# One more product of the setup by nested Strassen, in a new order, and four sums of W1 moved

## The chip, the cores and the metric

The kernel runs on one core of a Trainium2 chip. The metric is the time of one execution on the device in microseconds (us), the median of a few runs. Engines: TensorE (PE in the profile, its weight loads PEld), VectorE (DVE), ScalarE (ACT), GpSimd (POOL) and SyncE (SP), which issues most of the DMAs. All data are 32-bit floats.

## The reference

Shapes: x is 8 x 1024 x 1024, the context 8 x 64 x 512; D = 1024.

```python
mp = einsum('bme,de->bmd', ctx, W_mem)                 # 8 x 64 x 1024
scores = einsum('bnd,bmd->bnm', x, mp) / sqrt(D)
attn = softmax(scores)
mc = einsum('bnm,bmd->bnd', attn, mp)
gate = sigmoid(concat([x, mc], -1) @ W_gate.T + b_gate)
out = rmsnorm(x + gate * mc, norm_w)
```

With W_gate.T cut into an upper half W1 (for x) and a lower half W2 (for mc), the argument of the sigmoid is x W1 + attn (mp W2) + b. The kernel multiplies mp by W2 once, in the setup, and adds b there.

## The kernel before, in words

**Setup** (the first 79 us of the span). The context and W_mem come in, TensorE multiplies them by Strassen's scheme into mp transposed, kept as four tiles `m11, m12, m21, m22` of 128 x 4 x 256. Then mp W2 is formed by Strassen's scheme in Winograd's form, with seven products, into `c11, c12, c21, c22`, which go to DRAM (`store_mg`). Its left operands are `m11`, `m12`, `m22` and the sums `s1 = m21 + m22`, `s2 = s1 - m11`, `s3 = m11 - m21` and a fourth in s2's place; its right operands are the quarters `b11..b22` of W2 and sums of them: `t1 = b12 - b11`, `t2 = b22 - t1`, `b12` replaced by `b22 - b12`, `b21` replaced by `b21 - t2`. The products are:

1. m11 b11, 2. m12 b21 (the plain one), 3. (m12 - s2) b22, 4. m22 b21 (the replaced one), 5. s1 t1, 6. s2 t2, 7. s3 b12.

A dense product (`mg_product`) is 8 matmuls of 512 columns into two PSUM banks. Product 5 is nested (`second_product`): it is itself done by the same scheme, 7 inner products of two 256-column matmuls, with four sums of left quarters (`second_left`, on VectorE, tile `mg_left`), four sums of right quarters (`second_sum`, on GpSimd, tile `mg_right`), copies between banks on ScalarE and two adds into the banks on VectorE. A function given as `between` is issued ahead of the last inner product. The order before is 1, 5, 2, 6, 7, 4, 3. PSUM bank pairs are `up`, `side` and `both` (in the profile `pm_af`, `pm_ed` and `pm_ctx` in some order, with `mg_u` for the two inner banks). Product 1 is needed in most results: it is copied to `both`, and product 6 is accumulated on it.

In the same stretch VectorE and GpSimd make the weights of the main part: `outer_sum` (a sum of two 128 x 2048 quarters of W1, VectorE) and `inner_sum` (128 x 512, mostly GpSimd), which fill the `t{o}` and `it{o}` tiles; and the first quad of x is transposed on VectorE (`transpose_x`).

**Main part.** x is worked on in 16 quads of 512 rows. For each quad x W1 is formed by seven outer products in the order `ORDER = (1, 6, 7, 5, 4, 2, 3)`, each nested into seven inner products (banks `af`, `ed`, `kB`, `kC`). After the third inner product of outer products 4 and 3 stand the visits, which add attn (mp W2) (`pc`). Other work is laid in by hand: `at(slot, ...)` puts it ahead of the inner product of that number (49 to a quad), `mid((q, o, n), ...)` at places inside an outer product; `mid((0, 4, 0), ...)` comes right after the visits of outer product 4 of the first quad. The left sums of the next outer product (`inner_s`) are made on GpSimd. Each engine takes its instructions strictly in the order in which the program issues them (`keep_in_program_order`), and an instruction that waits holds up all behind it on its engine. All `tensor_tensor` sums carry line 96 and all matmuls line 93 in the profile, since one helper issues them.

Of the kernel before, what the change touches and what calls it, by code (L numbers as in the profile page):

```python
# [8 lines left out]
F32 = mybir.dt.float32  # L9
# [11 lines left out]
def tile_gated_cross_attention_rmsnorm(  # L21
# [73 lines left out]
    def tt(eng, o, a, b, op):  # L95
        pin(eng.tensor_tensor(o, a, b, op))  # L96
# [51 lines left out]
    def load_xq(q):  # L148
        b, n0 = q // QPB, (q % QPB) * QT
        xq[q] = t4k(xqpool, [P, 16, Q4], "xq", f"xq{q}")  # L150
        src = x[b, n0 : n0 + QT, :].rearrange("(s c) (i e) -> i c s e", c=32, i=4)
        for i in range(4):
            load(xq[q][32 * i : 32 * (i + 1), :, :], src[i])
# [58 lines left out]
    def outer_sum(o, a, b, k=slice(0, 4)):  # L212
        tt(nc.vector, outer_b[o][:, k], outer_b[a][:, k], outer_b[b][:, k], ALU.subtract)

    def inner_sum(eng, o, n):
        s, a, b = ((T1, R12, R11), (T2, R22, T1), (R12, R22, R12), (T4, R21, T2))[n]
        tt(eng, w_op(o, s), w_op(o, a), w_op(o, b), ALU.subtract)

    def inner_sums(eng, o):
        w1_place(o)  # L220
        for n in range(4):
            inner_sum(eng, o, n)
# [94 lines left out]
    def w2_sum(eng, o, a, b):  # L317
        for k in range(KH):
            tt(eng, o[k], a[k], b[k], ALU.subtract)

    def second_right(r, tag):

        r11, r21 = (r[:, 2 * k : 2 * k + 2, 0:C] for k in range(2))
        r12, r22 = (r[:, 2 * k : 2 * k + 2, C:H] for k in range(2))
        t = const.tile([P, 3, 2, C], F32, tag=tag, name="mg_right")
        return r11, r21, r12, r22, *(t[:, i, :, :] for i in range(3))

    def second_sum(eng, right, n):
        r11, r21, r12, r22, t4, t1, t2 = right
        o, a, b = ((t1, r12, r11), (t2, r22, t1), (t4, r21, t2), (r12, r22, r12))[n]  # L330
        tt(eng, o, a, b, ALU.subtract)

    right5 = second_right(t_w2[0], "it3")
    for k in range(KH):
        tt(nc.gpsimd if k > 1 else nc.vector, t1[k], b12[k], b11[k], ALU.subtract)
    for n in range(3):
        second_sum(nc.gpsimd, right5, n)
    w2_sum(nc.gpsimd, t2, b22, t1)
    second_sum(nc.gpsimd, right5, 3)
    pm_sum(m22, m22, up)  # L340
    outer_sum(5, 7, 1)
    w2_sum(nc.gpsimd, b12, b22, b12)
    inner_sums(nc.gpsimd, 1)

    pm_product(both, ps4, e22)
    pm_copy(m21, both)
# [190 lines left out]
    def store_mpT(r, h):  # L537
        load(mpd[:, h * KH : (h + 1) * KH, r * HM : (r + 1) * HM], mpT[r][h])
# [4 lines left out]
    def mp_step(eng, tag, pool, a, b, op):  # L543
        t = t4k(pool, [P, KH, HM], tag, f"mp_{tag}")
        tt(eng, t, a, b, op)
        return t
# [14 lines left out]

    def first_rows():

        t = const.tile([P, 2, Q4], F32, tag="it4", name="rows0")
        for h in range(2):
            pin(
                nc.vector.transpose(
                    chunks(t, KD)[:, h * KH : (h + 1) * KH], mpT[0][h][:, :, 0:M]
                )
            )  # L570
        store_rows(0, t)
# [10 lines left out]
    def mg_product(l, r, pgs, start=False):  # L582
        for t in range(2):
            for k in range(KH):
                mm(pgs[t], l[:, k, t * P : (t + 1) * P], r[k], start and k == 0, k == KH - 1)

    def second_left(eng, l, tag):

        l11, l12, l21, l22 = quarters(l)
        t = const.tile([P, 5, 2, P], F32, tag=tag, name="mg_left")  # L590
        s1, s2, s3, s4, zs = (t[:, i, :, :] for i in range(5))
        tt(eng, s1, l21, l22, ALU.add)
        tt(eng, s2, s1, l11, ALU.subtract)
        tt(eng, s3, l11, l21, ALU.subtract)
        tt(eng, s4, l12, s2, ALU.subtract)
        return l11, l12, l22, s1, s2, s3, s4, zs.rearrange("p k c -> p (k c)")

    def second_product(left, right, pgs, between):

        l11, l12, l22, s1, s2, s3, s4, zs = left  # L600
        r11, r21, r12, r22, t4, t1, t2 = right
        top, low = pgs
        u2 = bank("b", [P, C], "mg_u2")
        z = u3 = bank("c", [P, C], "mg_u3")

        def product(o, l, r, start=False):
            for k in range(2):
                mm(o, l[:, k, :], r[:, k, :], start and k == 0, k == 1)

        product(u2, l11, r11, True)  # L610
        pin(nc.scalar.copy(top[:, 0:C], u2))
        product(z, s1, t1, True)
        pin(nc.scalar.copy(zs, z))
        product(u2, s2, t2)
        pin(nc.scalar.copy(u3, u2))
        product(top[:, 0:C], l12, r21)
        tt(nc.vector, top[:, C:H], u2, zs, ALU.add)
        product(u3, s3, r12)
        pin(
            nc.scalar.copy(  # L620
                low.rearrange("p (n c) -> p n c", c=C), u3.unsqueeze(1).to_broadcast([P, 2, C])
            )
        )
        product(top[:, C:H], s4, r22)
        between()
        product(low[:, 0:C], l22, t4)
        tt(nc.vector, low[:, C:H], low[:, C:H], zs, ALU.add)

    def mg_tile(pool, tag, name):
        return t4k(pool, [P, 2, H], tag, name)  # L630

    def mg_copy(o, pgs):
        for t in range(2):
            pin(nc.scalar.copy(o[t] if isinstance(o, list) else o[:, t, :], pgs[t]))
# [5 lines left out]
        )  # L640

    s1 = mp_step(nc.vector, "s1", apool, m21, m22, ALU.add)
    store_mpT(0, 1)
    load_xq(0)
    c11 = mg_tile(rot, "u", "mg_c11")
    c12 = mg_tile(rot, "u", "mg_c12")
    c21 = mg_tile(rot, "l2", "mg_c21")
    c22 = mg_tile(small, "mg", "mg_c22")
    up, side = side, up
    mg_product(m11, b11, up, True)  # L650
    mg_copy(both, up)
    left5 = second_left(nc.vector, s1, "it6")

    def left6():
        nonlocal s2
        s2 = mp_step(nc.vector, "s2", apool, s1, m11, ALU.subtract)

    s2 = None
    second_product(left5, right5, side, left6)
    mg_copy(c22, side)  # L660
    outer_sum(7, 3, 7)
    w1_place(7)
    for n in range(4):
        inner_sum(nc.gpsimd, 7, n)
    mg_product(m12, b21, up)
    mg_copy(c11, up)
    store_mg(c11, 0, 0)
    first_rows()
    load_mp(0)
    s3 = mp_step(nc.vector, "junk", small, m11, m21, ALU.subtract)  # L670
    for t in range(4):
        transpose_x(0, t, 0)
    for part in range(2):
        inner_s(0, 1, part)
    w2_sum(nc.vector, b21, b21, t2)
    mg_product(s2, t2, both)
    mg_copy(c21, both)
    tt(nc.gpsimd, s2, m12, s2, ALU.subtract)
    for t in range(2):
        tt(nc.vector, side[t], c21[:, t, :], side[t], ALU.add)  # L680
# [94 lines left out]
    for n in (2, 3):  # L775
        at(4, inner_sum, nc.gpsimd, 4, n)
    for i, (o, n) in enumerate((o, n) for o in (2, 3) for n in range(4)):
        if i > 5:
            mid((0, 4, 0), inner_sum, nc.vector, o, n)
        else:  # L780
            at((3, 4, 5, 6, 14, 14)[i], inner_sum, nc.vector, o, n)
    slot = 0

    def step():
# [412 lines left out]
```

## Time and profile before

| what | us |
|---|---|
| median of 3 runs (945.33 to 946.3) | 946.27 |
| the profiled execution | 946.12 |
| its span | 943.5 |
| TensorE busy | 932.2 |
| VectorE busy | 803.7 |
| GpSimd busy | 738.1 |
| ScalarE busy | 432.6 |
| first matmul of the main part starts at | 78.88 |

How to read it: the span runs from the first to the last instruction of the profiled execution; its own time holds 2.6 us more around the span. Times in rows are microseconds from the start of the span. Matmuls are pipelined, and each row's duration reaches past the start of the next, so the time of a product is read from start to start.

### The profile page before, as it was taken

What the parts mean: (1) busy time and instruction counts of PE and PEld (TensorE: products, weight loads), DVE (VectorE), ACT (ScalarE), POOL (GpSimd) and SP (SyncE); (2) the same over time, 40 slices, a digit from 0 to 9 for tenths busy, and PEclk for the clock granted to TensorE, in tenths of its full rate; (3) what the DMA queues carried; (4) which work ended last, traced back from release to release, by engine and by line L of the source; (5) the groups of instructions that cost most, each with busy time, mean ns of one, the idle gap of its engine ahead of it and who ended that gap; (6) DMA issues with size and microseconds to landing.
All of it is one profiled execution on the core that took longest, in us unless ns stands there. A gap on an engine that the chain in (4) does not pass through costs nothing.

```text
span 943.5 us, 15920 instructions
## 1 busy us (share of the span) xinstructions
PE 932.2 (99%) x5572; PEld 727.7 (77%) x5572; DVE 803.7 (85%) x1267; ACT 432.6 (46%) x1111; POOL 738.1 (78%) x814
## 2 busy tenths in 40 slices
PE   9999999999999999999999999999999999999995
PEld 8646778787877778787877778687877778787774
DVE  6798988888897888888897888888897889888887
ACT  4212336273644527263644627263543627264556
POOL 4998978689686868778696868778696868878695
PEclk9999999999999999999999999999999999999998
DMA  9927294582919365481919366491918466491632
GB/s 378 310 69 157 47 162 115 125 178 51 206 57 185 103 137 125 118 183 44 214 57 179 90 145 135 101 201 33 221 60 168 101 136 144 93 205 31 137 151 89
DMA packets 71183, 128.43 MB, mean 136 GB/s; under 512 B 12608, under 2 KB 49472, under 8 KB 70848
## 3 DMA queue, kind: packets, MB, share of 16 engines
q1 hardware_dynamic: 61920, 93.86, 37.9%
q0 software_dynamic: 9184, 33.56, 19.6%
q8 instruction: 44, 0.72, 0.3%
q14 instruction: 35, 0.29, 0.1%
HBM read 87.56 MB, written 41.68 MB: 137 GB/s over the span
## 4 chain that ended last, share of the span: by engine, by line
PE 94%; DVE 3%; POOL 1%; issue 1%; DMA 1%; ACT 0%; SPq 0%; POOLq 0%; DVEq 0%; ACTq 0%
PE af L93 31%; PE ed L93 20%; PE kC L93 10%; PE kB L93 10%; PE pc L93 9%; PE psT_af L93 5%; PE pm_ctx L93 3%; PE pm_af L93 2%; PE pm_ed L93 2%; DVE gate L96 1%; POOL gate L96 1%; DMA wm<-in_w_mem_t 1%; PE psT_ed L93 0%; DVE u L96 0%; PE mg_u L93 0%
## 5 line engine op out<-in xcount | busy, mean ns | idle before, releaser
L96 POOL TENSOR_TENSOR gate<-gate,u 128x512 f32<-128x512 f32 (+1 forms) x224 | 245.3, 1108 | 151.3 <-DVE u L96 150.3
L795 ACT ACTIVATE gate<-gate 128x512 f32<-128x512 f32 x127 | 80.0, 630 | 183.2 <-DVE gate L96 181.7
L365 DVE STREAM_TRANSPOSE a<-xq 128x512 f32<-128x512 f32 x128 | 141.8, 1111 | 8.8 <-PE af L93 7.9
L96 POOL TENSOR_TENSOR l<-a 128x256 f32<-128x256 f32 x128 | 112.6, 880 | 17.3 <-PE af L93 15.8
L93 PE MATMUL pc<-mg,attnT 64*64 64x512 f32 x512 | 117.0, 596 | 0.3 <-DVE u L96 0.3
L93 PE MATMUL kB<-it,l 128*128 128x256 f32 x448 | 115.0, 379 | 0.0
L93 PE MATMUL ed<-it,l 128*128 128x256 f32 x448 | 115.0, 379 | 0.0
L824 DVE SCALAR_TENSOR_TENSOR gate<-gate,ss,nw_sb 128x512 f32<-128x512 f32 x120 | 110.3, 919 | 1.1
L93 PE MATMUL af<-w,a 128*128 128x256 f32 x384 | 98.5, 379 | 0.0
L1049 ACT COPY u<-af 128x256 f32<-128x256 f32 x112 | 41.5, 371 | 122.9 <-PE af L93 112.1
L96 DVE TENSOR_TENSOR gate<-gate,pc 128x512 f32<-128x512 f32 x128 | 85.5, 677 | 11.8 <-ACT gate L795 11.8
L93 PEld LDWEIGHTS kB<-it,l 128*128 128x128 f32 x448 | 85.0, 190 | 11.8 <-issue 0.2
L93 PEld LDWEIGHTS ed<-it,l 128*128 128x128 f32 x448 | 85.1, 190 | 11.6
L96 DVE TENSOR_TENSOR gate<-gate,ed 128x512 f32<-128x512 f32 x112 | 76.4, 682 | 16.6 <-POOL gate L96 14.6
L96 DVE TENSOR_TENSOR gate<-gate,af 128x512 f32<-128x512 f32 (+1 forms) x128 | 76.0, 603 | 12.0 <-PE af L93 10.5
L96 POOL TENSOR_TENSOR l<-s 128x256 f32<-128x256 f32 x96 | 84.5, 881 | 1.2 <-issue 1.2
L93 PEld LDWEIGHTS af<-w,a 128*128 128x128 f32 x384 | 73.0, 190 | 10.3 <-issue 0.5
L93 PEld LDWEIGHTS pc<-mg,attnT 64*64 64x64 f32 x512 | 32.8, 132 | 50.0 <-issue 23.2
L93 PE MATMUL ed<-it,a 128*128 128x256 f32 x256 | 67.4, 386 | 0.0
L93 PE MATMUL af<-mg,attnT 64*64 64x512 f32 (+1 forms) x380 | 67.0, 457 | 0.0
L96 DVE TENSOR_TENSOR u<-u,kB 128x256 f32<-128x256 f32 x112 | 45.9, 410 | 24.7 <-PE kB L93 23.5
L93 PE MATMUL af<-t,s 128*128 128x256 f32 x256 | 65.8, 379 | 0.0
(213 smaller groups left out, 2131.9 us busy)
## 6 DMA issues: line engine op xcount, KB each, us to landing
xq<-in_x SPq DMA_DIRECT2D x64, 512.0 KB, 10.0
gate<-in_x POOLq DMA_DIRECT2D x60, 512.0 KB, 8.2
out<-gate SPq DMA_DIRECT2D x60, 512.0 KB, 3.0
w<-in_w_gate_t SPq DMA_DIRECT2D x8, 512.0 KB, 10.2
w<-in_w_gate_t SPq DMA_DIRECT2D x2, 2048.0 KB, 17.2
mg<-mgd SPq DMA_DIRECT2D x16, 256.0 KB, 4.6
wm<-in_w_mem_t SPq DMA_DIRECT2D x4, 512.0 KB, 6.1
mpd<-mpT SPq DMA_DIRECT2D x4, 512.0 KB, 9.4
```

Of the source, the lines that this page charges most:

```text
L93: pin(nc.tensor.matmul(o, lhsT, rhs, start=start, stop=stop, skip_group_check=True))
L96: pin(eng.tensor_tensor(o, a, b, op))
L365: nc.vector.transpose(A[key][:, :, r * P : (r + 1) * P], chunks(xq[q][:, 4 * t : 4 * t + 4, :], KD)[:, half * KH : (half + 1) * KH],)
L795: pin(nc.scalar.activation(g, g, AF.Sigmoid))
L824: nc.vector.scalar_tensor_tensor(g[:, cols], g[:, cols], rstd[:, t % 2 : t % 2 + 1], nw_sb[:, cols], ALU.mult, ALU.mult,)
L1049: pin(nc.scalar.copy(p1, af[:, 0]))
```

## The change

In the setup product 6 (s2 t2) is now nested too. It gets right sums of its own on GpSimd (`sums6`; the fourth goes to a tile of its own, `spare`, because t2 is still needed as a whole), left sums of its own on VectorE (`left_sums6`), and runs into empty banks `both`; product 1 is copied to `c21` and added to `both` afterwards by two adds on VectorE. The order becomes 1, 5, 6, 2, 7, 4, 3. s2 is made right after s1; the sums of `b12` and of W1's outer product 1 come behind `sums6` on GpSimd; s3 comes ahead of product 6, W1's outer sum 7 into the middle of it; the rows of the first batch, the load of its mp and the first four transposes of x come ahead of product 2.

In the first quad, the four inner sums of W1 for outer product 3 stand at slots 12, 13, 14 and 14 instead of 14, 14 and twice after the visits of outer product 4.

```diff
-    def second_right(r, tag):
+    def second_right(r, tag, t3=None):
...
-        return r11, r21, r12, r22, *(t[:, i, :, :] for i in range(3))
-
-    def second_sum(eng, right, n):
-        r11, r21, r12, r22, t4, t1, t2 = right
-        o, a, b = ((t1, r12, r11), (t2, r22, t1), (t4, r21, t2), (r12, r22, r12))[n]
-        tt(eng, o, a, b, ALU.subtract)
-
-    right5 = second_right(t_w2[0], "it3")
+        t1, t2, t4 = (t[:, i, :, :] for i in range(3))
+        t3 = r12 if t3 is None else t3
+        sums = (t1, r12, r11), (t2, r22, t1), (t4, r21, t2), (t3, r22, r12)
+        return (r11, r21, t3, r22, t4, t1, t2), sums
+
+    def second_sums(eng, sums):
+        for o, a, b in sums:
+            tt(eng, o, a, b, ALU.subtract)
+
+    spare = const.tile([P, 3, 2, C], F32, tag="it4", name="spare")
+    right5, sums5 = second_right(t_w2[0], "it3")
+    right6, sums6 = second_right(t_w2[1], "it2", spare[:, 1, :, :])
...
-    for n in range(3):
-        second_sum(nc.gpsimd, right5, n)
+    second_sums(nc.gpsimd, sums5[:3])
     w2_sum(nc.gpsimd, t2, b22, t1)
-    second_sum(nc.gpsimd, right5, 3)
+    second_sums(nc.gpsimd, sums5[3:])
+    second_sums(nc.gpsimd, sums6)
     pm_sum(m22, m22, up)
     outer_sum(5, 7, 1)
-    w2_sum(nc.gpsimd, b12, b22, b12)
-    inner_sums(nc.gpsimd, 1)
...
-        t = const.tile([P, 2, Q4], F32, tag="it4", name="rows0")
+        t = spare[:, 0, :, :]
...
     s1 = mp_step(nc.vector, "s1", apool, m21, m22, ALU.add)
+    s2 = mp_step(nc.vector, "s2", apool, s1, m11, ALU.subtract)
     store_mpT(0, 1)
     load_xq(0)
+    lt5 = const.tile([P, 5, 2, P], F32, tag="it6", name="mg_left5")
+    lt6 = t4k(rot, [P, 4, 2, P], "l2", "mg_left6")
+    left5, left_sums5 = second_left(s1, lt5, lt5[:, 4, :, :].rearrange("p k c -> p (k c)"))
+    left6, left_sums6 = second_left(s2, lt6, spare[:, 2, 0, :])
...
     mg_product(m11, b11, up, True)
-    mg_copy(both, up)
-    left5 = second_left(nc.vector, s1, "it6")
-
-    def left6():
-        nonlocal s2
-        s2 = mp_step(nc.vector, "s2", apool, s1, m11, ALU.subtract)
-
-    s2 = None
-    second_product(left5, right5, side, left6)
+    mg_copy(c21, up)
+    left_sums5(0, 1, 2, 3)
+    left_sums6(0)
+    second_product(left5, right5, side, lambda: left_sums6(1, 2, 3))
     mg_copy(c22, side)
-    outer_sum(7, 3, 7)
+    s3 = mp_step(nc.vector, "junk", small, m11, m21, ALU.subtract)
+    w2_sum(nc.gpsimd, b12, b22, b12)
+    inner_sums(nc.gpsimd, 1)
+    second_product(left6, right6, both, lambda: outer_sum(7, 3, 7))
     w1_place(7)
     for n in range(4):
         inner_sum(nc.gpsimd, 7, n)
+    for t in range(2):
+        tt(nc.vector, both[t], c21[:, t, :], both[t], ALU.add)
+    mg_copy(c21, both)
+    first_rows()
+    load_mp(0)
+    for t in range(4):
+        transpose_x(0, t, 0)
     mg_product(m12, b21, up)
     mg_copy(c11, up)
     store_mg(c11, 0, 0)
-    first_rows()
-    load_mp(0)
-    s3 = mp_step(nc.vector, "junk", small, m11, m21, ALU.subtract)
-    for t in range(4):
-        transpose_x(0, t, 0)
     for part in range(2):
         inner_s(0, 1, part)
     w2_sum(nc.vector, b21, b21, t2)
-    mg_product(s2, t2, both)
-    mg_copy(c21, both)
...
-        if i > 5:
-            mid((0, 4, 0), inner_sum, nc.vector, o, n)
-        else:
-            at((3, 4, 5, 6, 14, 14)[i], inner_sum, nc.vector, o, n)
+        at((3, 4, 5, 6, 12, 13, 14, 14)[i], inner_sum, nc.vector, o, n)
```

More of the change, by code (lines that the diff above doesn't have):

```diff
@@ L585, in mg_product, with second_left, sums @@
                 mm(pgs[t], l[:, k, t * P : (t + 1) * P], r[k], start and k == 0, k == KH - 1)
-    def second_left(eng, l, tag):
+    def second_left(l, t, zs):
         l11, l12, l21, l22 = quarters(l)
[L590 to L596, printed above, removed]
+        s1, s2, s3, s4 = (t[:, i, :, :] for i in range(4))
+        def sums(*which):
+            for n in which:
+                o, a, b, op = (
+                    (s1, l21, l22, ALU.add),
+                    (s2, s1, l11, ALU.subtract),
+                    (s3, l11, l21, ALU.subtract),
+                    (s4, l12, s2, ALU.subtract),
+                )[n]
+                tt(nc.vector, o, a, b, op)
+        return (l11, l12, l22, s1, s2, s3, s4, zs), sums
     def second_product(left, right, pgs, between):
```

## The prediction

> **What bounds the kernel now.** I read the page's busy shares first, then the list of who waited for whom, for TensorE, then the setup stage engine by engine in the timeline.
>
> ```profile
> PE 932.2 (99%) x5572; PEld 727.7 (77%) x5572; DVE 803.7 (85%) x1267; ACT 432.6 (46%) x1111; POOL 738.1 (78%) x814
> PE pc L93 <- DVE u L96: 0.3, 1, 0.3
> ```
>
> The first row is the page's busy time, the second TensorE's only wait after its start, 0.3 us in the whole span: TensorE is the bound. So a matmul removed is worth its full time, and every wait added to TensorE is paid in full, because nothing later can take it up again. All that the change can bring is matmuls saved plus that 0.3 us. What it can cost is decided by the queues that feed TensorE in the setup. Their rows (start, duration, then in brackets the idle time before it):
>
> ```profile
> 30.31 2.29 DVE L96 TENSOR_TENSOR mp_s<-mpT,mpT 128x1024 f32<-128x1024 f32 x1
> 32.64 1.37 DVE L96 TENSOR_TENSOR mg_left<-mp_s 128x256 f32<-128x256 f32 x1
> ...
> 36.74 1.48 DVE L96 TENSOR_TENSOR mg_left<-mp_s,mg_left 128x256 f32<-128x256 f32 x1
> 42.17 0.43 DVE L96 TENSOR_TENSOR pm_af<-mg_u,mg_left 128x256 f32<-128x256 f32 x1 [3.94 <-PE pm_af L93]
> 42.51 1.60 DVE L96 TENSOR_TENSOR mp_s<-mp_s,mpT 128x1024 f32<-128x1024 f32 x1
> 44.82 0.43 DVE L96 TENSOR_TENSOR pm_ed<-pm_ed,mg_left 128x256 f32<-128x256 f32 x1 [0.71 <-PE pm_ed L93]
> 45.16 2.28 DVE L96 TENSOR_TENSOR w<-w,w 128x2048 f32<-128x2048 f32 x1
> 47.36 1.11 DVE L567 STREAM_TRANSPOSE rows<-mpT 128x256 f32<-128x256 f32 x2
> 48.31 1.35 DVE L96 TENSOR_TENSOR mp_junk<-mpT,mpT 128x1024 f32<-128x1024 f32 x1
> 49.70 4.10 DVE L365 STREAM_TRANSPOSE a<-xq 128x512 f32<-128x512 f32 x4
> 53.71 6.36 DVE L96 TENSOR_TENSOR w<-w,t_w 128x512 f32<-128x512 f32 x4
> 59.99 0.68 DVE L96 TENSOR_TENSOR pm_af<-mg_c,pm_af 128x512 f32<-128x512 f32 x1
> 60.59 0.68 DVE L96 TENSOR_TENSOR pm_ed<-mg_c,pm_ed 128x512 f32<-128x512 f32 x1
> 61.19 2.42 DVE L96 TENSOR_TENSOR t<-w,t 128x2048 f32<-128x2048 f32 x1
> 63.53 0.67 DVE L96 TENSOR_TENSOR mg_c<-mg_c,pm_ctx 128x512 f32<-128x512 f32 x1
> ```
>
> ```profile
> 38.44 1.03 PE L93 MATMUL mg_u<-t_w,mp_s 128*128 128x256 f32 x4
> ...
> 44.55 3.60 PE L93 MATMUL pm_af<-w,mpT 128*128 128x512 f32 x8
> ...
> 51.42 7.03 PE L93 MATMUL pm_ctx<-t_w,mp_s 128*128 128x512 f32 x16
> 58.28 7.03 PE L93 MATMUL pm_ctx<-w,mp_junk 128*128 128x512 f32 x16
> 65.15 7.03 PE L93 MATMUL pm_ctx<-w,mpT 128*128 128x512 f32 x16
> ```
>
> The products of the setup stand here in the order 1, 5 (38.44), 2 (44.55), 6 (51.42), 7 (58.28), 4 (65.15), 3. See two things. VectorE has no idle time at all from 44.82 to the last row at 63.53, although product 7 had filled the first bank that this row adds by 58.28 + 3.43 = 61.7 (half of the 6.87 between the starts of products 7 and 4): VectorE already runs behind. And product 4 overwrites that bank: the add ends at 64.2, product 4 starts at 65.15. The margin is 0.95 us. Whatever lengthens VectorE's queue ahead of that add by more than the margin becomes a wait of TensorE.
>
> **The change, part by part.**
>
> TensorE: product 6 dense takes 58.28 - 51.42 = 6.86. Product 5, already nested, takes 44.55 - 38.44 = 6.11 with its one small gap; seven inner products of half a dense row's width. By the ratio 7 to 8 of the work it would be 6.00, 0.86 for an inner product. I take 6.05, a saving of 0.8, which puts product 4 at 64.35 if nothing waits.
>
> VectorE, in its new order. s2 is made right after s1: I take s1's 2.29, 32.64 + 2.29 = 34.9. The four left sums of product 5 were spaced 1.40 (32.64 to 38.22 with the last one's duration): to 40.5. The first left sum of product 6: 41.9. That all lies in the old idle time of 3.94, and the add at 42.17 waits for TensorE as before; product 5 is fed in time. From 42.51 on the sums are:
> - three left sums of product 6, put between the parts of product 5 where s2 (1.60) was: 3 x 1.40, to 46.7. The add at 44.82 stands behind them on VectorE and now starts at 46.7, ends at 47.1;
> - s3, 1.35 as at 48.31: to 48.5;
> - product 6's first PSUM add. For it see TensorE below: not before 50.2, to 50.5;
> - W1's outer sum (2.20 from 45.16 to 47.36): to 52.75; product 6's last add, 0.43: 53.15;
> - the two adds of product 1 into product 6's banks, new, spaced 0.60 like 59.99 and 60.59: to 54.35;
> - rows (0.95 to 48.31): 55.3; four transposes (4.01 to 53.71): 59.3; four sums of b21 (6.28 to 59.99): 65.6; two adds 1.20: 66.8; outer sum (2.34 to 63.53): 69.1; the add that frees product 4's bank, 0.6: 69.75.
>
> Why 1.40 for a left sum and not less: GpSimd ran sums of its own from 31.48 on without a gap, and these VectorE sums kept GpSimd's pace.
>
> ```profile
> 25.62 1.28 POOL L96 TENSOR_TENSOR mg_right<-t_w 128x512 f32<-128x512 f32 x1 [1.45 <-DVE t_w L96]
> 26.98 4.54 POOL L96 TENSOR_TENSOR mg_right<-t_w,mg_right 128x512 f32<-128x512 f32 x2
> 31.48 6.46 POOL L96 TENSOR_TENSOR t_w<-w,t_w 128x512 f32<-128x512 f32 x4
> ...
> 82.31 0.73 POOL L96 TENSOR_TENSOR l<-s 128x256 f32<-128x256 f32 x1 [1.21 <-issue]
> 83.11 1.11 POOL L96 TENSOR_TENSOR l<-l,s 128x256 f32<-128x256 f32 x1
> ```
>
> A 128x512 add that reads PSUM took 0.68 beside the same GpSimd work (59.99), one whose inputs both lie in SBUF 1.57 (6.28 / 4 from 53.71). Between 26.98 and 82.31 no row of GpSimd has idle time, and its queue gets longer, so I keep the contended values. Bounds for a left sum: 0.43, as for the add of this size that reads PSUM (42.17), and 1.48.
>
> ScalarE and TensorE in product 6:
>
> ```profile
> 45.28 0.59 ACT L634 COPY mg_c<-pm_ed 128x512 f32<-128x512 f32 x1 [0.88 <-DVE pm_ed L96]
> ```
>
> The second copy of c22 waits for VectorE's add (44.82 then, 46.7 now), and product 6's first copy out of its bank stands behind it on ScalarE. The third inner product writes that bank again. So: add ends 47.1, copy of c22 (0.59) to 47.8, copy of the bank, of half the width and so some 0.35, to 48.15, third inner product at 48.2 instead of 44.55 + 2 x 0.86 = 46.27. A wait of 1.9 us; product 6 then ends at 48.2 + 5 x 0.86 = 52.5, its first PSUM add is free at 50.2 (two inner products on, and 0.2 as at 42.17), product 2 ends at 59.4, product 7 at 66.2. Product 4 starts when the bank is free, at 69.85: a second wait of 3.6 us. The b21 sums need product 2's reads, over at 59.4, and start at 59.3 anyway.
>
> Product 4 starts 69.85 - 65.15 = 4.7 later than before, with the saved 0.8 already inside.
>
> GpSimd: four more 128x512 sums, 1.28 each (the row at 25.62; together 5.1) to 1.62 (6.46 / 4), and about 1 us for s2 moved beside its work: 6.1 to 7.5 late. Before them it was done at 39.3 (31.48 + 6.46 + one more sum of 1.4), now at 40.4; at 1.44 each they end from 41.8 to 46.1, each ahead of its inner product (45.4, 46.3, 48 and 49.7 at the earliest). Later GpSimd is 1.4 to 2.8 behind a TensorE that is itself 4.7 late. Cover: the left sum ready at 84.2 is first used by the matmul at 89.60 (below), 5.4 us. I cost it at nothing.
>
> DMA: the four row stores and the load of mp now go ahead of c11's store on SP's queue. The first reader of what c11's store writes is the load of mg, which sits behind c12's store, after product 3; that one shifts with TensorE. Nothing waits longer than TensorE is late: nothing. Buffers (l2, it2, it4) are taken over only after product 6 has ended, and their next writers come later than 55: nothing.
>
> First quad: two of W1's inner sums leave the place after the visits, two come ahead to slot 12 and 13.
>
> ```profile
> 110.00 1.38 DVE L96 TENSOR_TENSOR w<-w 128x512 f32<-128x512 f32 x1
> 111.30 3.16 DVE L96 TENSOR_TENSOR it<-w,it 128x512 f32<-128x512 f32 x1
> ```
>
> ```profile
> 89.60 1.03 PE L93 MATMUL kB<-it,l 128*128 128x256 f32 x4
> ...
> 125.94 0.65 PE L93 MATMUL pc<-mg,attnT 64*64 64x512 f32 x2 [0.33 <-DVE u L96]
> ```
>
> The chain of waits leads from the 4.46 us of sums at 110.00 over the gate steps to the wait at 125.94. Taking them away should remove it: 0.33 (bounds 0 and 0.33). Two sums come two slots and one slot ahead of the two that stood at slot 14 already, where TensorE never waited; the worst would be a wait of the size that goes (0.33). I take nothing: the PSUM banks that VectorE has to empty there are each written again only seven inner products of 0.86 later.
>
> **Sum**, against the profiled execution: 946.12 (span 943.5 plus 2.62 around it; the median of the three runs is 946.27, 0.15 above) + 4.7 - 0.33 = 950.5. Lower bound: left sums at 0.43 end by 43.9, the add at 44.82 and the c22 copy stay where they were, product 6 doesn't wait; its first PSUM add is then at 48.25, and the same queue (0.35, 2.20, 0.4, and 16.6 from the two adds on) frees the bank at 67.8, product 4 starts at 67.9: +2.75 - 0.33, 948.5. Upper bound: s3 at 2.29, the outer sums at 2.88 (2.28 plus the 0.6 that a GpSimd sum can hold it) and 3.4, the b21 sums at 1.75, left sums at 1.48: 3.4 more, 953.9.
>
> **A rule against the trace.** Two waits of TensorE, 1.9 and 3.6 us, are longer than any in this trace, so no row here shows what follows one. What a TensorE fresh from rest does, a row shows, with the granted clock of the 40 slices ahead of it:
>
> ```profile
> PEclk9999999999999999999999999999999999999998
> ```
>
> ```profile
> 1.19 3.78 PE L93 MATMUL pz<-zeros 128*128 128x256 f32 x8 [1.19 <-DVE zeros L116]
> ```
>
> Eight instructions in 3.78 us are 0.47 each, where product 5's inner products, of the same width, take 0.86 for four; the page grants TensorE the same clock, nine tenths or more, in that slice as in those that follow, so the row shows the slow pace but not its cause. If the second wait brings that pace back for as long, some 3.6 us of work takes twice the time it should and 1.8 us is lost. The Trainium skill, TensorE: Matmul & The Clock Gate, section Why this matters for your kernels, asks for no gaps over about 3 us between matmuls, since one idle window puts the clock back to half. By that rule the sum would be 952.3, by the rows without it 950.5. That is a rival below.
>
> **Rivals.**
> - *VectorE is not held up, and TensorE never waits* (the other side). Place: the left sums at 42.6 and the b21 sums. If they run at the pace of the adds from PSUM (0.43 and 0.68 instead of 1.40 and 1.57), the bank is free at 67.8 of the lower bound less 4 x 0.89 = 64.2, just ahead of the 64.35 from which it decides. Then 946.12 - 0.8 - 0.33 = 945.0. Against it: GpSimd's unbroken queue. 0.17, with what ends between this and 0.2% slower.
> - *The clock falls back after the wait*: 952.3. For it the slow first row; against it that the first wait is shorter than the 3.78 us which that row took to warm up, and the second no longer. 0.12.
> - *GpSimd becomes the bound*: its four sums cost 2.25 each, as the two at 26.98 did (4.54), it falls some 10 us back, 5.4 more than TensorE, and product 6 of the first quad waits for its left sums: about 1 us more, 951.5. 0.08.
> - *The forecast*: 0.60, own range 948.5 to 953.5; 0.02 of it at the low end falls within 0.2%. Left: 0.03 for a gain over 0.2%, for which the sum has no term.
>
> A measurement of this kernel tells 0.2%, 1.9 us, from no change. Faster by that: 0.03, since 0.8 + 0.33 is all there is to gain. Within: 0.17 + 0.02 = 0.19. Slower: 0.78. The range for 8 in 10 is 946.5 to 953.4: most of the first rival below it and the end of the forecast's own range above it are left out.
>
> **What would show it.** In the changed profile: a wait of TensorE of 1 to 2 us at about 46 in the third inner product of product 6, behind ScalarE's copies; a wait of 3 to 4 us before product 4, put down to VectorE's add to c22; VectorE without idle time from 50 to 70; product 4 at 69 to 71; no wait at the visits near 126 + 4.4. Wrong it would be if VectorE's left sums and b21 sums take 0.43 and 0.68 us beside a busy GpSimd, or if VectorE runs its queue in another order than written.

## The result, and the profile after

| | before | changed |
|---|---|---|
| median of 6 runs each, us | 946.21 (945.33 to 946.30) | 953.72 (952.80 to 954.49) |
| profiled execution, us | 946.12 | 954.49 |
| its span, us | 943.5 | 952.7 |

The ratio is 1.0081, 95% interval 1.0068 to 1.0094: 7.5 us slower. The forecast was 950.5, range 946.5 to 953.4. The sign is right, the size is not, and the time lies 0.3 us above the range.

From the page after: the busy row, the granted clock in 40 slices, and the shares of the chain that ended last.

```profile
PE 935.2 (98%) x5584; PEld 730.7 (77%) x5584; DVE 808.5 (85%) x1275; ACT 434.1 (46%) x1115; POOL 742.9 (78%) x818
PEclk9998999999999999999999999999999999999998
PE 89%; DVE 5%; POOL 3%; DMA 2%; issue 1%; ACT 1%; SPq 0%; POOLq 0%; DVEq 0%; ACTq 0%
```

Although one product was made cheaper, TensorE is busy 3.0 us longer than before (932.2), and the fourth slice of the clock (71 to 95 us) is an 8. TensorE's waits after the change (total, times, longest), beside the single 0.3 of before:

```profile
PE pm_ctx L93 <- DVE mg_c L96: 4.2, 1, 4.2
...
PE mg_u L93 <- POOL w L96: 1.0, 1, 1.0
PE af L93 <- ACT u L1057: 0.8, 1, 0.8
PE pm_af L93 <- POOL pm_it L284: 0.4, 1, 0.4
```

Where they stand, in TensorE's timeline (start, duration, idle time before):

```profile
44.73 1.03 PE L93 MATMUL mg_u<-t_w,mp_s 128*128 128x256 f32 x4
...
47.58 1.10 PE L93 MATMUL mg_u<-mg_right,mg_left 128*128 128x256 f32 x4 [0.96 <-POOL w L96]
...
52.04 3.60 PE L93 MATMUL pm_af<-w,mpT 128*128 128x512 f32 x8
...
70.13 10.18 PE L93 MATMUL pm_ctx<-w,mpT 128*128 128x512 f32 x16 [4.20 <-DVE mg_c L96]
80.14 3.60 PE L93 MATMUL pm_af<-w,mp_s 128*128 128x512 f32 x8
...
87.01 1.03 PE L93 MATMUL af<-w,a 128*128 128x256 f32 x4
```

Product 6 runs from 44.73 to 52.04 with a wait of 0.96 in its third inner product. Product 4 starts at 70.13 instead of 65.15 and then takes 10.01 from start to start where it took 6.87. The reason stands in the clock column (the number after the five engines' busy times) of a table by stretches; the last two columns are the DMA's share and GB/s:

```profile
65.50:70.13 4.63, 0.43 (x2) 0.00 (x0) 4.63 (x6) 0.00 (x0) 4.55 (x4) 0.93 0.00 0
70.13:72.00 1.87, 1.87 (x3) 0.84 (x3) 1.87 (x2) 0.00 (x0) 1.87 (x2) 0.50 0.22 81
72.00:74.00 2.00, 2.00 (x4) 0.97 (x3) 0.90 (x1) 0.00 (x0) 2.00 (x1) 0.50 0.50 186
74.00:76.00 2.00, 2.00 (x3) 0.72 (x3) 0.86 (x1) 0.00 (x0) 2.00 (x2) 0.50 0.00 0
76.00:78.00 2.00, 2.00 (x6) 0.78 (x4) 1.25 (x2) 0.59 (x1) 1.92 (x3) 0.93 0.00 0
```

The granted clock falls to 0.50 at about 69.5, before the rest of 4.2 us is over, and stays there for the first 6.2 us of product 4, up to 76.3. So the main part begins at 87.01, 8.13 late: 4.98 (the start of product 4; 0.18 of it stands ahead of the stage already) + 3.14 (its slow pace). In the first quad the wait of 0.82 comes on top, about 1.0 from start to start, and the 0.33 at the visits is gone: 8.8. The span grew by 9.2, and the 0.4 between the two I can't place: the last matmul starts 9.12 late (941.96, before the change 932.84), 0.2 of it added in the last quad, where the profile names no wait. The profiled execution's time grew by 8.4, since the time around the span was 0.8 shorter. It is the longest of its six runs; the median is 0.8 below it.

VectorE's queue after the change:

```profile
43.35 1.49 DVE L96 TENSOR_TENSOR mg_left<-mp_s 128x256 f32<-128x256 f32 x1
44.76 1.49 DVE L96 TENSOR_TENSOR mg_left<-mp_s,mg_left 128x256 f32<-128x256 f32 x1
46.17 0.42 DVE L96 TENSOR_TENSOR pm_ed<-pm_ed,mg_left 128x256 f32<-128x256 f32 x1
...
59.32 6.63 DVE L96 TENSOR_TENSOR w<-w,t_w 128x512 f32<-128x512 f32 x4
...
67.07 2.41 DVE L96 TENSOR_TENSOR t<-w,t 128x2048 f32<-128x2048 f32 x1
69.40 1.27 DVE L96 TENSOR_TENSOR mg_c<-mg_c,pm_ctx 128x512 f32<-128x512 f32 x2
```

The add that frees product 4's bank starts at 69.40 and takes 0.6 of the 1.27 for two: 70.0, where the prediction said 69.75. And ScalarE, at product 6's wait, which the list of waits puts down to GpSimd: the copy out of the bank, stuck behind the second copy of c22, ends at 47.49, 0.09 ahead of the matmul.

```profile
46.62 0.59 ACT L642 COPY mg_c<-pm_ed 128x512 f32<-128x512 f32 x1 [2.03 <-DVE pm_ed L96]
47.11 0.38 ACT L619 COPY pm_ctx<-mg_u 128x256 f32<-128x256 f32 x1
```

### The profile page after: what moved, and what is told of

Its sections match the earlier page's. It is cut to its first block, busy times and chain, and to the rows that moved or that the text cites. A ratio compares the mean times of both kernels' runs of the same rounds, so it can differ in the third digit from the quotient of the medians.

```text
span 952.7 us, 15968 instructions
## 1 busy us (share of the span) xinstructions
PE 935.2 (98%) x5584; PEld 730.7 (77%) x5584; DVE 808.5 (85%) x1275; ACT 434.1 (46%) x1115; POOL 742.9 (78%) x818
## 4 chain that ended last, share of the span: by engine, by line
PE 89%; DVE 5%; POOL 3%; DMA 2%; issue 1%; ACT 1%; SPq 0%; POOLq 0%; DVEq 0%; ACTq 0%
PE af L93 30%; PE ed L93 20%; PE pc L93 10%; PE kC L93 10%; PE kB L93 10%; PE psT_af L93 5%; PE pm_ctx L93 1%; POOL gate L96 1%; PE pm_af L93 1%; DMA xq<-in_x 1%; DVE gate L96 1%; PE pm_ed L93 1%; DVE w L96 1%; POOL mg_right L96 1%; POOL l L96 1%
```

## The experiments

Each time is a median, beside a ratio to runs of the kernel before on the same chip (its medians there: 945.4 to 945.7).

### The moved sums of the first quad

**e1**: the changed kernel with the slots of before. **e2**: the kernel before with the new slots alone.

```diff
-        at((3, 4, 5, 6, 12, 13, 14, 14)[i], inner_sum, nc.vector, o, n)
+        if i > 5:
+            mid((0, 4, 0), inner_sum, nc.vector, o, n)
+        else:
+            at((3, 4, 5, 6, 14, 14)[i], inner_sum, nc.vector, o, n)
```

> The changed kernel with its first-quad part undone: the four inner sums of W1 for outer product 3 stand again at slots 14, 14 and twice after the visits. Theory (the moved sums delay the softmax on VectorE, which is what TensorE waited for at 114.25): the 0.82 us wait goes, the 0.33 us wait at the visits comes back, so 0.5 us less than the changed kernel, about 953.2. Rival (VectorE was late there because of the late setup, not because of the sums): the 0.82 us wait stays, the 0.33 comes back, 954.0.

> The kernel before with the first-quad part alone: the sums at slots 12, 13, 14 and 14, the setup untouched. Theory (the sums delay the softmax): a new wait of about 0.8 us in outer product 7 or 5 of the first quad, the 0.33 at the visits gone: 946.7. Rival (harmless by itself): no new wait, the 0.33 gone, 945.9.

e1: 952.20, 1.0074 [1.0062, 1.0087]. e2: 946.28, 1.0010 [1.0001, 1.0019], 0.8 above its before. So the slot part by itself costs some 0.8 us, net of the 0.33 that it does take away. The mechanism, three views. First VectorE in the kernel before, then in e2:

```profile
97.02 1.10 DVE L96 TENSOR_TENSOR it<-w,it 128x512 f32<-128x512 f32 x1
98.04 0.69 DVE L96 TENSOR_TENSOR den<-den 128x8 f32<-128x8 f32 x1
```

```profile
98.85 0.68 DVE L96 TENSOR_TENSOR w<-w 128x512 f32<-128x512 f32 x1
99.45 1.21 DVE L96 TENSOR_TENSOR it<-w,it 128x512 f32<-128x512 f32 x1
100.59 0.15 DVE L96 TENSOR_TENSOR den<-den 128x8 f32<-128x8 f32 x1
```

The two sums moved ahead stand directly in front of the softmax's denominators, which come 2.55 us later, 2.25 of it from the sums (all in e2 starts 0.3 late). What follows on ScalarE and TensorE in e2:

```profile
101.01 1.80 ACT L493 ACTIVATE sc<-sc,den 128x32 f32<-128x32 f32 x8 [3.76 <-DVE den L488]
...
105.91 0.36 ACT L1046 COPY u<-af 128x256 f32<-128x256 f32 x1
```

```profile
106.41 1.10 PE L93 MATMUL af<-t,l 128*128 128x256 f32 x4 [0.81 <-ACT u L1046]
```

ScalarE waits for the denominators, its copies of the attention come later, and behind them stands the copy that empties the bank `af` (at 103.90 before). TensorE needs that bank: 0.81 us.

### The slow pace after the rest

**e3, e5, e12**: idle matmuls of 128x256 into an unused bank ahead of product 4, 8, 3 and 4 of them, so that the rest gets shorter while product 4 still starts when VectorE lets it.

```diff
+    warm = bank("b", [P, C], "warm_b")
+    for _ in range(8):
+        mm(warm, m22[:, 0, 0:P], b11[0][:, 0:C], True, True)
     mg_product(m22, b21, both)
```

> The changed kernel with eight idle matmuls (128x256, into a PSUM bank that nobody reads) ahead of product 4, some 3.5 us of work inside the 4.2 us wait. Theory (the slow product 4 comes of the rest ahead of it): product 4 still starts at about 70.1, but takes 6.9 us from start to start instead of 10.0 and the granted clock of that stretch is 1.00: 3.1 us less, 950.6. Rival (product 4 is slow for its operands, its weight loads or the VectorE and GpSimd work beside it): it still takes 10.0 us, no change of the time.

> The changed kernel with three idle matmuls (1.3 us) ahead of product 4, so that TensorE rests for about 2.9 us there instead of 4.2. Theory (the clock falls only after a rest as long as a fixed window, some 3.4 us by the page on the clock gate): product 4 takes 6.9 us from start to start at a granted clock of 1.00, the time is that of the run with eight, 0.6% above the kernel before. Rival (the clock falls after any rest of 2 to 3 us): product 4 takes 9 to 10 us, 0.8% above the kernel before, as the changed kernel.

> The changed kernel with four idle matmuls (1.7 us) ahead of product 4, so that TensorE rests for about 2.5 us. Seen so far: rests of 1.6 and 1.9 us cost nothing more, one of 2.9 cost 1.8 us of slow pace, 4.2 cost 3.1. Theory (whether the clock falls depends on how the rest lies to a window, so a rest between these falls in some executions only): the runs spread by more than 1 us, between 951.5 and 953.5 on a kernel before of 945.5. Rival (a threshold between 1.9 and 2.5): slow pace in all, 952.5 to 953.5. Rival (a threshold between 2.5 and 2.9): in none, 951.5 with a spread below 0.5.

e3: 951.48, 1.0064 [1.0051, 1.0078]. TensorE, and the clock of the same stretch (0.50 in the changed kernel from 70 to 75):

```profile
65.56 3.62 PE L93 MATMUL warm_b<-w,mpT 128*128 128x256 f32 x16
69.92 7.13 PE L93 MATMUL pm_ctx<-w,mpT 128*128 128x512 f32 x16 [0.74 <-DVE mg_c L96]
```

```profile
70.00:75.00 5.00, 5.00 (x12) 2.30 (x13) 2.76 (x3) 0.58 (x1) 5.00 (x3) 1.00 0.28 105
```

Product 4 starts as late as before the filling, and takes 6.97: the slow pace comes of the rest, not of the product. The medians differ by less than the profiles: the changed kernel is 7.5 above its before, e3 6.0 above its own, so the pace costs about 1.5 in the median run, by this difference, and 3.1 in the profiled one, by its rows.

e5: 952.75, 1.0073 [1.0058, 1.0088]. The rest is 2.90, product 4 takes 1.8 us too long, and the clock falls, but only at 71.0, when product 4 has been running for 1.1 us:

```profile
69.92 8.83 PE L93 MATMUL pm_ctx<-w,mpT 128*128 128x512 f32 x16 [2.90 <-DVE mg_c L96]
```

```profile
70.00:75.00 5.00, 5.00 (x8) 2.13 (x9) 2.77 (x3) 0.00 (x0) 5.00 (x3) 0.66 0.28 105
```

e12: 952.19, 1.0069 [1.0055, 1.0083]; the rest is 2.49, and its four runs are 951.5, 951.6, 952.8 and 952.9. The profiled one, 951.58, kept full clock:

```profile
70.00 7.13 PE L93 MATMUL pm_ctx<-w,mpT 128*128 128x512 f32 x16 [2.49 <-DVE mg_c L96]
```

Over their whole span the two shorter ones were granted a mean clock of 0.998, the two others 0.995 and 0.994. So the theory of e5, that only a longer rest lowers the clock, fell: a rest of 2.5 to 2.9 us loses it in some executions and not in others, for 1.3 to 1.8 us.

### The order of VectorE's queue

**e4**: the two adds to c22 ahead of W1's outer sum 6 (2.4 us). **e6**: the fourth left sum of product 6 behind the add that c22's copy waits for.

```diff
-    outer_sum(6, 3, 5)
-    for n in range(4):
-        inner_sum(nc.gpsimd, 5, n)
     mg_product(s3, b12, both)
     for t in range(2):
         tt(nc.vector, c22[:, t, :], c22[:, t, :], both[t], ALU.add)
     store_mg(c22, 1, 1)
+    outer_sum(6, 3, 5)
+    for n in range(4):
+        inner_sum(nc.gpsimd, 5, n)
```

```diff
-    second_product(left5, right5, side, lambda: left_sums6(1, 2, 3))
+    second_product(left5, right5, side, lambda: left_sums6(1, 2))
+    left_sums6(3)
```

> The changed kernel with the two adds to c22 ahead of W1's outer sum 6 on VectorE instead of behind it. Theory (product 4 waits for VectorE's queue, whose last term before the bank is free is this outer sum of 2.33 us): product 4 starts at 67.8, after a wait of 1.9 us, and, the rest being shorter, at the full clock: 2.3 + 3.1 = 5.5 us less, 948.3. Rival (product 4 waits for something else, such as the b21 sums): these end at 65.95, so the wait would be almost nothing, 946.2. Rival (the clock falls after a rest of 1.9 us too): 951.4.

> The changed kernel with the fourth left sum of product 6 put behind product 5's last add on VectorE, so that the c22 copy and product 6's third inner product are not held up. Theory (every wait ahead of product 4 is absorbed by the wait there, since VectorE's queue alone sets when it starts): the 1.0 us wait in product 6 goes, product 4's start stays at 69.5 to 70.1, its wait grows to about 5 us, its slow stretch stays; the time changes by less than 0.5 us. Rival (the waits add up): 1.0 us less.

e4: 951.21, 1.0061 [1.0047, 1.0075]. The wait before product 4 falls to 1.85 and there is no slow pace, but TensorE now waits 1.3 for ScalarE (`af`) and 1.3 for VectorE (`kB`) in the first quad: the span is 3.3 us shorter than the changed kernel's, of 5.5 expected, and most of the difference went into these waits (2.6 in the place of 0.8). e6: 952.56, 1.0073 [1.0058, 1.0088]. The wait in product 6 is gone, product 4 starts at 68.87, 1.26 earlier (some 0.2 of it because the whole setup stands earlier), behind a rest of 4.27; my theory had it unmoved.

**e7**: e6 with the slots of before, the sums of b21 ahead of the transposes and the adds to c22 early. **e11**: e7 with GpSimd's m12 - s2 ahead of the weights of outer product 7. **e9**: e6 with the slots of before and the four sums of b21 left out (product 4 then multiplies the plain b21).

```diff
-    for t in range(4):
-        transpose_x(0, t, 0)
     mg_product(m12, b21, up)
...
     w2_sum(nc.vector, b21, b21, t2)
...
     mg_product(s3, b12, both)
     tt(nc.vector, c22[:, 0, :], c22[:, 0, :], both[0], ALU.add)
+    for t in range(2):
+        transpose_x(0, t, 0)
     tt(nc.vector, c22[:, 1, :], c22[:, 1, :], both[1], ALU.add)
...
+    outer_sum(6, 3, 5)
...
+    for t in (2, 3):
+        transpose_x(0, t, 0)
```

> The changed kernel with the sums of b21 ahead of the first transposes, the adds to c22 ahead of W1's outer sum 6, the fourth left sum as in the run before this one, and the first-quad sums at their old slots: the same work in an order that serves product 4 first. Theory A (VectorE and GpSimd have more to do in this stretch than TensorE, and an order only moves the wait): no wait at product 4, product 4 at 64.5, but waits of 3 us or more in the first quad, whose left sums and adds come later; 0.3% above the kernel before, 948.5 on its chip time of 945.5. Rival B (the order alone was at fault): no waits at all, 0.8 us below the kernel before.

> The changed kernel with the first-quad sums at their old slots, the fourth left sum as above, and the four sums of b21 left out (product 4 multiplies with the unreplaced quarter): 6.6 us of VectorE's work is gone, nothing else. Theory (the nested product 6 is worth its 0.8 us to TensorE as soon as VectorE has the room): product 4 starts without a wait at 64.4 to 64.7, and the time is 0.8 us below the kernel before. Rival (GpSimd's four added sums are a bound of their own): waits remain in the first quad, for left sums made on GpSimd, and the time is at or above the kernel before.

> The reordered kernel with GpSimd's sum for product 3 put ahead of W1's inner sums 7, nothing left out: the attempt at an order without waits in the setup. Theory (both queues have more to do than TensorE's time allows, until the slack of the first quad): no wait at products 4 and 3, but 2 to 3 us of waits in the first quad, for VectorE's adds or GpSimd's left sums; 1.5 us above the kernel before. Rival (there is room, only the order was wrong): 0.8 us below the kernel before.

e7: 951.28, 1.0057 [1.0042, 1.0072]. Product 4 has no wait any more, and product 3 gets one, for GpSimd, with a slow pace behind it:

```profile
75.22 5.24 PE L93 MATMUL pm_af<-w,mp_s 128*128 128x512 f32 x8 [3.56 <-POOL mp_s L96]
```

e9: 948.05, 1.0026 [1.0016, 1.0036]. With 6.6 us of VectorE's work gone the time is still not that of before: product 3 waits 1.61 for the same sum on GpSimd. My theory, which put the whole loss on VectorE, fell here. e11: 950.10, 1.0046 [1.0034, 1.0059]. The setup runs almost without waits (0.2 us ahead of product 4; outer product 1 at 78.71, 0.17 earlier than before), and the first quad pays instead:

```profile
PE af L93 <- ACT u L1063: 1.3, 1, 1.3
...
PE psT_b L93 <- DVE u L96: 0.9, 1, 0.9
PE kC L93 <- DVE sT L96: 0.7, 1, 0.7
PE pc L93 <- DVE u L96: 0.6, 2, 0.4
```

Three orders, three places for the wait. What is pushed along is work, so the next runs leave work out.

### Whose work is too much

**e10**: e7 without GpSimd's four right sums of product 6, which reads those of product 5 instead.

```diff
-    second_sums(nc.gpsimd, sums6)
...
-    second_product(left6, right6, both, lambda: outer_sum(7, 3, 7))
+    second_product(left6, right5, both, lambda: outer_sum(7, 3, 7))
```

> The reordered kernel with GpSimd's four right sums of product 6 left out (its inner products read product 5's right sums instead), all else as there. In the reordered kernel product 3 waited 3.6 us for a sum of GpSimd. Theory (behind VectorE's queue GpSimd's is the next bound, late by the four added sums): that sum is done some 6 us sooner, product 3 does not wait, the first outer product starts at 78.3, and the time is 0.8 us or less below the kernel before (at most 1 us of waits comes back in the first quad, where VectorE is still late). Rival (the sum is late because VectorE holds it up, not because of the four sums): product 3 still waits 2 us or more, 0.3% or more above the kernel before.

949.54, 1.0040 [1.0026, 1.0054]. Product 3 still waits 2.61, with a slow pace behind it (5.23 us from its start to that of its second half, instead of 3.43): in e7's order GpSimd stands idle 5.08 us for the late transposes, so that order was a poor base. I took a better one.

**e14**: the changed kernel with e4's and e6's orders and the slots of before, nothing left out. **e15**: e14 without VectorE's four left sums of product 6 and two adds. **e16**: e14 without GpSimd's four right sums. **e17**: without either. In e15 to e17 product 6 reads product 5's sums where its own are missing; TensorE's instructions are the same in all four.

```diff
-    left_sums6(0)
...
-    for t in range(2):
-        tt(nc.vector, both[t], c21[:, t, :], both[t], ALU.add)
```

> Base of the three runs after it: the changed kernel with three orders mended, nothing left out: the adds to c22 ahead of W1's outer sum 6, the fourth left sum behind product 5's last add, the first-quad sums at their old slots. Theory (VectorE and GpSimd have too much to do together): product 4 starts near 66.8 after a rest of 2 us, 2 to 3 us of waits in the first quad, about 950, 0.5% above the kernel before. Rival (orders were all): near the kernel before.

> That base with VectorE's added sums left out: the four left sums of product 6 (it reads product 5's) and the two adds of product 1 into its banks. GpSimd's four right sums stay. Theory (VectorE's added time is the cause): product 4 starts without a wait at 64.4 to 64.8, and the time is within 1 us of the kernel before, either way. Rival (GpSimd's added time holds up VectorE and TensorE by itself): 2 us or more above the kernel before, with waits in the first quad for left sums.

> That base with GpSimd's four right sums of product 6 left out (its inner products read product 5's), VectorE's added sums kept. Theory (VectorE's added time is the cause): product 4 still waits 1 us or more, 2 us or more above the kernel before. Rival (GpSimd's added time is the cause): no waits, 0.8 us below the kernel before. If both share it: between, 946 to 947.5.

> That base with both left out: the nested product 6 without any sums of its own, so that VectorE and GpSimd have what they had in the kernel before, but for two adds into inner banks. Theory: TensorE's saving shows: no wait of more than 0.5 us at products 4 and 3 and in the first quad, 0.4 to 0.8 us below the kernel before. Rival (the order of products 1 5 6 2 7 4 3 costs by itself): waits of 1 us or more remain, at or above the kernel before.

| left out | time, us | ratio, 95% | waits before products 4, 3 |
|---|---|---|---|
| nothing (e14) | 950.08 | 1.0047 [1.0031, 1.0064] | 1.47, 1.46 |
| VectorE's sums (e15) | 949.72 | 1.0045 [1.0030, 1.0060] | 0, 2.56 |
| GpSimd's sums (e16) | 945.34 | 0.9994 [0.9985, 1.0003] | 0, 0 |
| both (e17) | 944.93 | 0.9991 [0.9982, 1.0001] | 0, 0 |

By the medians, VectorE's new work is worth 0.4 us in this order, whether GpSimd's stands (950.08 - 949.72) or not (945.34 - 944.93), and GpSimd's 4.7 or 4.8. The first 0.4 is what is left of a larger gain. Without VectorE's sums the wait before product 4 goes, but the one before product 3 grows, and in the profiled run of e15 a slow pace follows it:

```profile
74.33 5.40 PE L93 MATMUL pm_af<-w,mp_s 128*128 128x512 f32 x8 [2.56 <-POOL mp_s L96]
```

The first half of product 3 takes 5.23 us from start to start, in e14 3.54: some 1.7 us of what e15 gained in that run went into the clock. So the agreement of the two 0.4 says little. That GpSimd's sums are what counts rests on e16, where no wait is left before either product though all of VectorE's new work stands.

The interval of e17 just touches 1, so its 0.8 us below before can't be told from no change by the times alone. But it is what product 6's saving had been put at, and the rows show that saving: product 6 takes 6.14 us there (44.84 to 50.98) instead of 6.86. GpSimd's rows tell why its sums cost so much: its sum m12 - s2 (`mp_s`), product 3's left operand, and the sum ahead of it, in e14 and then in e16.

```profile
69.87 2.77 POOL L96 TENSOR_TENSOR l<-a,l 128x256 f32<-128x256 f32 x1
72.60 2.34 POOL L96 TENSOR_TENSOR mp_s<-mpT,mp_s 128x1024 f32<-128x1024 f32 x1
```

```profile
62.21 1.17 POOL L96 TENSOR_TENSOR l<-a,l 128x256 f32<-128x256 f32 x1
63.34 2.36 POOL L96 TENSOR_TENSOR mp_s<-mpT,mp_s 128x1024 f32<-128x1024 f32 x1
```

9.3 us later, for four sums that take some 5.8 us: the rest is GpSimd held up by VectorE's sums that it now runs beside, as in the 128x256 sum of 2.77 us instead of 1.17. It goes the other way too, in VectorE's four sums for b21, e14 and then e16:

```profile
57.90 6.65 DVE L96 TENSOR_TENSOR w<-w,t_w 128x512 f32<-128x512 f32 x4
```

```profile
57.76 5.04 DVE L96 TENSOR_TENSOR w<-w,t_w 128x512 f32<-128x512 f32 x4
```

The Trainium skill, SBUF — State Buffer, section Who interferes with whom, says that a VectorE instruction with two inputs in SBUF contends with a GpSimd instruction that reads SBUF, since its second input comes through a read interface that the two engines share. These rows agree: the same sum takes 1.26 or 1.66 us on VectorE by what GpSimd does beside it.

**e18, e19**: the same two omissions, each alone, in the order of the changed kernel itself.

> The changed kernel in its own order, GpSimd's four right sums of product 6 left out (product 6 then reads those of product 5, so c21, c22 and c12 are not the reference's). Theory (in the changed order both engines' new work meets in VectorE's one queue ahead of the add to c22, and either of them alone makes product 4 wait): GpSimd comes some 5 us earlier, W1's and b21's sums on VectorE get 1.5 to 2 us shorter, the adds to c22 start at about 67, product 4 waits some 2 us instead of 4.2, perhaps with no slow pace behind it, and the slots cost 0.8 as before: 948 to 949 us where the changed kernel has 953.7. Rival (GpSimd's sums are the whole cause, as in the mended order): no wait before product 4, 945.5 to 946.5. Rival (VectorE's new work is the whole cause in this order): 952 to 954.

> The changed kernel in its own order, VectorE's four left sums of product 6 and the two adds of product 1 into its banks left out (product 6 reads product 5's left sums, c21, c22 and c12 are not the reference's). Theory (both engines' work meets in VectorE's queue): the queue ahead of the add to c22 is some 4 us shorter, the adds start at about 66.3, product 4 waits 1.5 to 2 us without a slow pace, GpSimd's m12 - s2 comes in time, the slots cost 0.8: 947.5 to 949. Rival (GpSimd's sums are the whole cause): GpSimd's m12 - s2 is as late as before, 952 to 954 by a wait before product 4 or 3. Rival (VectorE's work is the whole cause): 945.5 to 946.5.

e18: 951.36, 1.0063 [1.0046, 1.0080]. e19: 951.74, 1.0069 [1.0054, 1.0084]. Product 4 in e18, then in e19:

```profile
68.45 7.13 PE L93 MATMUL pm_ctx<-w,mpT 128*128 128x512 f32 x16 [2.87 <-DVE mg_c L96]
```

```profile
68.55 8.71 PE L93 MATMUL pm_ctx<-w,mpT 128*128 128x512 f32 x16 [3.62 <-DVE mg_c L96]
```

In that order neither is the cause alone: each, left out, brings product 4 forward by 1.6 or 1.7 us of 5.0. Both reach TensorE through VectorE's one queue ahead of the add to c22, GpSimd's sums by holding up VectorE's own. VectorE's four sums of b21 in e18, 6.63 us in the changed kernel:

```profile
58.98 4.46 DVE L96 TENSOR_TENSOR w<-w,t_w 128x512 f32<-128x512 f32 x4
```

No run leaves out both in that order. Both times come out 2.4 to 4.2 us above my expectation, since the waits were longer (I had put them at about 2) and the clock fell after them: in e19's profiled run it did; e18's profiled run, 949.64 with full clock, was the shortest of four, and the others, which have no trace, took 951.4.

### A way to keep the gain of the slot part

**e13**: the kernel before, one of the two late sums moved to GpSimd at slot 35.

```diff
-        if i > 5:
+        if i == 6:
+            at(35, inner_sum, nc.gpsimd, o, n)
+        elif i == 7:
             mid((0, 4, 0), inner_sum, nc.vector, o, n)
```

> The kernel before with one of the two inner sums that VectorE makes after the visits put on GpSimd at slot 35, in its idle time there; the other stays. Theory (the 0.33 us wait at the visits comes of VectorE's two sums): the wait goes and no other comes, 0.3 us below the kernel before, less than the runs can tell. Rival: GpSimd's adds come late instead and the wait stays or grows, same time or 0.5 us above.

945.08, 0.9996 [0.9987, 1.0005]. The wait at the visits is gone and no other came in its place in the first quad; 0.4 us, which can't be told from no change. No version run that computes everything is measurably faster than the kernel before.

## Why the prediction was right and wrong

- **TensorE bounds, and product 6's saving is 0.8**: right. In e17, which has the nested product and none of its new sums, product 6 takes 6.14 instead of 6.86, and the time is 0.8 below before, at the edge of what the runs can tell.
- **VectorE's queue as a clock**: right. Left sums of 1.40 took 1.41 from start to start (one only 0.7), b21's 6.28 measured 6.63, the freed bank at 69.75 came at 70.0, product 4 at 69.85 came at 70.13.
- **The wait in product 6 behind ScalarE's copy**: right in place and cause (e6 and e19 remove it), half in size: 0.96 instead of 1.9, since one left sum took 0.7 instead of 1.4. TensorE then waited so much longer before product 4; the sum of both was 5.2 instead of 5.5.
- **The clock after the rest**: this is the first step that failed. I gave the rival 0.12, on the ground that the second wait was "no longer" than the slow row at the start. The length of that row says how long a slow pace lasted there, not how long a rest has to be to bring one on. Rests of 2.5 to 2.9 us already lost it in some executions; the one here was 4.2. The 1.8 us of the rival was near the median loss (about 1.5, by e3), and below the 3.1 of the profiled run. The Trainium skill's rule, cited in the prediction, was right to warn. The Trainium skill, TensorE: Matmul & The Clock Gate, section What's actually happening, has the clock fall after an idle window of some 3.4 us and calls the number of slow matmuls at a kernel's start variable from run to run; the runs here agree that executions differ, but their clock fell after shorter rests too (2.56, 2.61 and 2.90 us in e15, e10 and e5).
- **"I take nothing" for the sums moved in the first quad**: the second step that failed. They cost 0.8 net instead of bringing 0.33 (e1, e2), a difference of 1.1. I looked at the PSUM banks that VectorE empties and not at the rest of its queue: behind the new sums stood the denominators, and behind these ScalarE's copy of a bank. "The worst would be a wait of the size that goes" had no row under it.
- **GpSimd's four sums at nothing**: the third step that failed, which the sum hid. I had seen that its queue has no idle time from 27 to 82 us and counted only its final lateness. In the mended order its sums alone cost 4.7 us (e16); in the changed order they are a third of product 4's lateness, and VectorE's new work is another third (e18, e19); what makes up the last third there no run shows. Product 4's start was forecast well all the same, because I had taken VectorE's sums at their durations beside a busy GpSimd, and so part of the price stood in my sum under VectorE's name (b21's four sums: 6.63, and 4.46 without GpSimd's in e18).

From 950.5: + 1.1 for the slots, + 1.5 for the clock in the median run, + 0.3 for product 4's start gives 953.4; the median is 953.72. The upper bound that the prediction worked out, 953.9, would have held, but it came of a slower VectorE, which is not what happened; its range left the end of that bound out. What stays open is why the loss of clock differs between executions, and the 0.4 us of the span.

## What to carry to other kernels

A saved piece of the bounding engine is worth taking only if the engines that prepare it have idle time in that stage: read the idle brackets of their queues first. In a full queue most of the new work's length came out at the first consumer that had no slack (4.7 us here, for sums of 5.8), and another order moved the waits more than it removed them. When work is moved ahead in a queue, follow everything behind it, small instructions too, to the engine that waits for them. And when a forecast has TensorE rest for more than about 2.5 us, add what these runs lost by the clock, 1.3 to 3.1 us, or fill the rest with idle matmuls, as in e3.

## What the hardware showed that I had not expected

The granted clock fell to 0.50 after rests of TensorE of 2.5 to 4.3 us, not after 0.7, 1.5, 1.6 or 1.9, and at 2.5 and 2.9 not in every execution, at a loss of 1.3 to 3.1 us. Read in stretches of 0.25 us, it stayed at 0.50 for one of two lengths: 3.41 us in e5, e7, e10, e15 and e19 (rests of 2.56 to 3.62), 6.83 us in the changed kernel, e1 and e6 (rests of 4.20, 4.19 and 4.27). It need not fall within the rest: in e10, e5 and e15 TensorE had been at work again for 0.4, 1.1 and 1.4 us. Half of 3.41 is 1.7, which is also the distance between the shortest and the longest of the changed kernel's runs; that these differ by one such stretch is not shown, since only the profiled one has a trace. Kernels with such a rest scatter more: the six runs of the changed kernel span 1.7 us, the four of e3, which fills the rest, 0.4. And one 128x256 sum on GpSimd took 1.17 or 2.77 us (e16, e14) by what VectorE did beside it.
